# A relational graph layer on one core: more tiles fetched row by row, later stores, an earlier first gather and a reordered end

## The chip, the core and the metric

The kernel runs on one core of one Trainium2 chip. The metric is the device time in microseconds (us) of one execution; lower is better. Several runs are made of a kernel and their median is compared. One more execution is taken by the hardware profiler, which gives the trace read here.

## What is computed

There are N = 12500 nodes with D = 256 features, E = 212500 edges sorted by destination, and R = 8 edge types with a 256x256 weight matrix each.

```python
h = jnp.maximum(_layernorm(x, axis=-1), 0.0)
hx = jnp.einsum('ni,rio->rno', h, weight)
msg = hx[edge_type, src]
agg = jax.ops.segment_sum(msg, dst, num_segments=num_nodes)
node_repr = agg * 0.5 ** 0.5 + h_bias
node_repr = node_repr + (h @ loop_weight) * 0.5 ** 0.5
return x + node_repr
```

The kernel first sums the source rows of each pair (destination, type) and multiplies by the weights afterwards. Both orders give the same result.

## The kernel before

**Tiles.** The edges are cut into units of about 271 and each unit into two tiles of 128 slots; there are 1578 tiles, numbered t. For each tile the 128 source rows (1 KB each) are brought into a tile `msg`. TensorE (PE) multiplies it with a 0/1 matrix made by VectorE (DVE), which sums rows by (destination, type): the "edge sums" of line 1036, four matmuls a tile, 6312 in all. DVE adds each unit's sums into a ring `acc` (L1069). A group of 128 nodes that is complete goes through 18 products with the weights (L1243, two of them the node's own row with `wl`, the "loops"); DVE adds x and the bias (L1231, L1258) and SyncE (SP) stores the rows (L1260 for single groups, L1263 for four groups at once). There are 98 groups.

**How the rows come in.** Most tiles are gathered by one indirect DMA that GpSimd (POOL) issues: L941, in `gather`. One tile in SINGLE (28) is instead "fetched": its 128 rows are copied by 128 plain DMAs of one row each (L970, `load_sources`), 64 issued by SP and 64 by ScalarE's queue (ACT). For every 32 rows the engine first loads 32 addresses into registers (L962, TENSOR_LOAD). PE waits for the rows of such a tile by a counter (L1033). Fetched tiles begin when their row table is normalised and stored in `h32`; gathers of earlier tiles read `x`, and DVE and ACT normalise these tiles in place (L830 to L874).

**Who may run ahead.** One loop over t writes all engines' instructions in one order; every engine executes its own in that order. At step t the gathers up to `goal(t)` are written, which is 64 tiles ahead (AHEAD) up to t = 170, then one tile less every 5 steps down to 24 (NEXT), and towards the end (1578 - t) // 5 down to 8 (CLOSE). Each gather also waits until the last finished unit ahead of its step is summed (L950). The `msg` tiles are a ring of 33 pairs. A fetched tile takes its pair of buffers FAR tiles ahead at the latest, its first rows are written HOLD (8) steps later, four instructions a step for each of the two queues.

**Around it.** Indices come in blocks of 128 units: SP loads `nat_s`, `nat_d` and `nat_t` (L407), then small "spans" transfers follow (L419), eight a block on ACT's queue, for the first such block on SP's. DVE turns them into gather addresses in some 70 small steps (`background`), and in the last block fills the unused part first (L402 to L404). The table of a block's source rows is `gidx`. For the first block it needs a load, a cast, a transposition on PE and a cast (L391, L468, L428, L432).

Of the kernel before, what the change touches and what calls it, by code (L numbers as in the profile page):

```python
# [12 lines left out]
I32 = mybir.dt.int32  # L13
# [47 lines left out]
NEXT = 24  # L61
CLOSE = 8

SINGLE = 28
FETCH = 4
SOURCES = 32
BY_SP = (0, 2)
HOLD = 8
FAR = 36
COUNTERS = 4  # L70
LANDINGS = 68

# [23 lines left out]
PREP = 232  # L96
LOADED = 20
EARLY = 30
SETTLE = 4
ROOM = 5  # L100
SHARE = 1.15
# [148 lines left out]
def kernel(  # L250
# [78 lines left out]
    with ExitStack() as main:  # L329
# [31 lines left out]
        added, zeroed, listed = {}, {}, set()  # L361
        single, fetches = {}, {SP: [], ACT: []}
        counters = [tc.alloc_semaphore(f"rows{i}") for i in range(COUNTERS)]
        fetched, summed = {}, {}
        landings = [tc.alloc_semaphore(f"landed{i}") for i in range(LANDINGS)]
# [17 lines left out]
                runs[kind] = (key, count)  # L383
            return i

        def load_indices(b):

            nat = {name: ep.tile([P, WIDE + 1], I32, name=f"nat_{name}") for name in "std"}
            if b == 0:
# [9 lines left out]
            nat["spans"] = small.tile([P, 2], I32, name="spans")  # L399
            if b == NB - 1:  # L400
                for name in "std":
                    nc.vector.memset(nat[name], N if name == "d" else 0)  # L402
                nc.vector.memset(nat["spans"][:, 0:1], 0)
                nc.vector.memset(nat["spans"][:, 1:2], N + SPAN - (E - spans[-1]))  # L404
# [10 lines left out]
            queue = nc.scalar if b > 1 else nc.sync  # L415
            for k, e in enumerate(spans):
                n = min(TURN, rows_ - k * TURN)
                both = 2 if e + SPAN < E else 1
                queue.dma_start(nat["spans"][k * TURN : k * TURN + n, :both], bass.AP(  # L419
                    tensor=dst.tensor, offset=dst.offset + e, ap=[[0, n], [SPAN, both]]))  # L420
            return nat

# [374 lines left out]
        def prepare(b):  # L797

            got = {}
            return [  # L800
                lambda: got.update(load_indices(b)), *sources(b, got), *last_edges(b, got),
                *columns(b, got), *places(b, got), *(verdict(got) if b == NB - 1 else [])]


# [105 lines left out]

        def single_rows(t):

            return (t % SINGLE == SINGLE - 1 and t + 2 * NEAR < NT
                    and state["h32"] is not None and t // QUAD * QUAD >= state["h32"] + LATE + AHEAD)

        def begin_fetch(t):

            if t not in msg:
                room(t - t % PAIR)
            fetched[t] = len(fetched)  # L920
            for k, r in enumerate(range(0, P, SOURCES)):
                engine = SP if k in BY_SP else ACT
                fetches[engine].append((
                    done["tile"] + HOLD,
                    lambda r=r, engine=engine: load_sources(t, r, engine)))

        def gather(t):
            if t % PAIR == 0 and t not in msg:
                room(t)
            if t % QUAD:  # L930
                kind[t] = kind[t - 1]
            else:
                kind[t] = "h" if state["h32"] is not None and t >= state["h32"] + LATE else "x"
# [7 lines left out]
            i = nc.gpsimd.indirect_dma_start(  # L941
                out=msg[t], out_offset=None, in_=table[:, :],
                in_offset=bass.IndirectOffsetOnAxis(ap=gidx[b][:, at : at + 1], axis=0))
# [269 lines left out]
        def wrap(g):  # L1213
# [3 lines left out]
            tc.add_manual_dep(i.ins, added[plan.last[g]].name, SYNC_DEP, reason="sums complete")  # L1217
            nc.vector.memset(acc[:, :, :, RING : RING + WIN], 0.0)

        def group_work(g):  # L1220

            d0 = plan.starts[g]
# [10 lines left out]
            def product(r, c, g=g):  # L1233
                n = plan.ends[g] - plan.starts[g]
                if (r, c) == (R, 0):
                    got["out", g] = outs[g % 2][:, 0, :]
                if r == R:
                    while ("self", g) not in got:
# [12 lines left out]
                    tc.add_manual_dep(i.ins, added[plan.last[g]].name, SYNC_DEP, reason="sums complete")  # L1251

            def finish():
                q, k = divmod(g, XG)
                rows_ = got["x", q]
                if g != final:
                    biased(g)
                nc.vector.tensor_add(rows_[:n, k, :], rows_[:n, k, :], got["out", g][:n])  # L1258
                if XG * (q + 2) >= plan.NG or n < P:
                    nc.sync.dma_start(out[d0 : d0 + n], rows_[:n, k, :])  # L1260
                elif k == XG - 1:
                    first = plan.starts[XG * q + shorts(q)]
                    nc.sync.dma_start(  # L1263
                        out[first : d0 + n].rearrange("(k p) d -> p k d", p=P), rows_[:, shorts(q) :, :])
                b = g + SLOTS
                q, k = divmod(b, XG)
                if b < plan.NG:
# [18 lines left out]
                    work.append((0.55, lambda r=r, c=c: product(r, c)))  # L1286
            work.append((0.0, last))
            if final is not None and g == final - 1:
                work.append((0.0, lambda: biased(final)))
                for c in range(KC):  # L1290
                    work.append((0.55, lambda c=c: product(R, c, final)))
            return work

        with tc.manual_schedule():

            load = prepare(0)
            load[0]()
            for i in range(STAGED):
                load_rows(i)
            make_identity(nc, ident)  # L1300
# [12 lines left out]
            for f in load[1 : 1 + head]:  # L1313
                f()
            for t in range(min(STARTED, NT)):
                gather(t)
            gathered = min(STARTED, NT)

# [34 lines left out]
            for i in range(2, FIRST):  # L1353
                norm_rows(i)
            after += close()
            for f in load[1 + head :]:
                f()
            after.pop(0)()
            ahead = prepare(1)
            ahead[0]()  # L1360
            nc.vector.memset(acc[:, :, :, RING:].rearrange("p c r d -> p (c r) d"), 0.0)
            for g in range(min(CLEARED, plan.NG)):
                clear(g)
# [28 lines left out]

            def blocks_ahead(t):
                for b in range(1, NB):
                    if t == max(0, PAIR * (RAW + P * (b - 1)) - PREP):
                        for k, f in enumerate(prepare(b) if b > 1 else ahead):
                            if b > 1 or k:
                                background.append((t + ((LOADED if b > 1 else EARLY) + k if k else 0), f))
                        background.sort(key=lambda a: a[0])

            begun = {}
# [44 lines left out]
            for t in range(NT):  # L1446
# [87 lines left out]
                step()  # L1534
            while held():
                advance(None)
            state["general"] = nc.values_load(flag[0:1, 0:1], min_val=0, max_val=1)
            while queue or late:
                if late:
                    late.pop(0)[1]()  # L1540
                else:
                    queue.pop(0)[3]()


    with tc.If(state["general"]):
# [26 lines left out]
```

## Time and profile before

| what | value |
|---|---|
| median of 3 runs | 1940.45 us (1939.35 to 1941.13) |
| the profiled execution, its own time | 1939.95 us |
| its span in the trace | 1938.2 us |
| mean granted TensorE clock | 0.955 |
| PE / DVE / POOL busy, share of the span | 87% / 68% / 75% |
| POOL gathers | 88 from `x`, 1440 from `h32` |
| rows fetched one by one | 3200 by SP, 3200 by ACT: 50 tiles |

The span is 1.75 us shorter than the execution's own time, and that time is 0.5 us below the median. A row of the timeline reads: start in us from the span's start, length in us (of the whole row, where instructions were merged), engine, line, operation, output<-input, count, and in brackets the engine's idle time before it with what ended it. A "q" behind an engine is its sequencer: the issuing of DMAs and loading of registers, which the busy shares leave out.

### The profile page before, as it was taken

To read this page: it belongs to the slowest core of one execution; us is meant where nothing else is said; L and a number is where in the kernel's file an instruction comes from. 1 tells how busy PE (TensorE), PEld (TensorE's weight loads), DVE (VectorE), ACT (ScalarE), POOL (GpSimd) and SP (SyncE) were. 2 spreads that over 40 slices of the span, in tenths; PEclk is the share of its full clock that TensorE was granted. 3 is DMA by queue.
4 is the path that set the end of the run, shared out by engine and by line. 5 is a ranking of instruction groups with operands and counts; after the bars stand their busy time and mean duration, and the time that the engine had idled before them with its cause. 6 is when DMAs were issued, how large, how long until landed. Compare 5 with 4: busy or idle time off the path is not lost.

```text
span 1938.2 us, 40494 instructions
## 1 busy us (share of the span) xinstructions
PE 1693.9 (87%) x10152; PEld 1455.2 (75%) x10152; DVE 1315.0 (68%) x3304; ACT 136.4 (7%) x290; POOL 1453.3 (75%) x1554
## 2 busy tenths in 40 slices
PE   2368999999898899889899989898898989899998
PEld 1357889899887787777777778677777778777887
DVE  7879668976667865657766557775566786565543
ACT  6974000000000000000000000000000000000000
POOL 7777777777777777777777777777777777777775
PEclk9568999999999999999999999999999999999999
DMA  9964444444454444453444444444444444444432
GB/s 319 385 216 138 138 132 131 142 134 143 121 154 131 121 142 131 122 150 111 141 132 121 141 132 130 134 118 142 131 120 136 128 135 132 123 141 127 132 118 87
DMA packets 158466, 279.13 MB, mean 144 GB/s; under 512 B 35487, under 2 KB 109330, under 8 KB 158226
## 3 DMA queue, kind: packets, MB, share of 16 engines
q0 software_dynamic: 73344, 200.38, 35.5%
q1 hardware_dynamic: 76744, 72.84, 12.0%
q10 hardware_dynamic: 8138, 3.30, 0.9%
q8 instruction: 80, 1.31, 0.3%
q14 instruction: 160, 1.31, 0.2%
HBM read 250.78 MB, written 25.60 MB: 143 GB/s over the span
## 4 chain that ended last, share of the span: by engine, by line
PE 37%; DMA 22%; POOL 19%; DVE 9%; issue 9%; ACT 3%; SPq 1%; DVEq 0%; POOLq 0%; ACTq 0%; PEldq 0%
DMA msg<-h,gidx 20%; POOL msg L941 19%; PE po L1243 19%; PE ps L1036 17%; DVE acc L1069 2%; ACT msg L874 1%; DVE oh L998 1%; DVE stats L830 1%; SPq L970 1%; DVE acc L1111 1%; ACT xt L874 1%; DVE moves L456 1%; DMA w<-in_L_gnn_weight_dram 1%; DMA xt<-in_x_dram 1%; PE pt L1093 1%
## 5 line engine op out<-in xcount | busy, mean ns | idle before, releaser
L941 POOL DMA_INDIRECT msg<-h,gidx x1440 | 1367.7, 950 | 439.9 <-issue 374.9
L1036 PEld LDWEIGHTS ps<-oh,msg 128*128 128x128 f32 x6312 | 924.9, 197 | 380.0 <-DMA msg<-h,gidx 247.0
L1036 PE MATMUL ps<-oh,msg 128*128 128x136 f32 (+1 forms) x6312 | 1001.9, 289 | 198.8 <-DMA msg<-h,gidx 122.9
L1243 PE MATMUL po<-w,acc 128*128 128x256 f32 (+1 forms) x3136 | 888.7, 389 | 8.7 <-DVE acc L1069 8.3
L1069 DVE TENSOR_TENSOR acc<-acc,ps 128x352 f32 x789 | 408.2, 517 | 387.5 <-PE ps L1036 376.6
L1243 PEld LDWEIGHTS po<-w,acc 128*128 128x128 f32 (+1 forms) x3136 | 519.1, 193 | 47.5 <-issue 11.9
L1111 DVE SCALAR_TENSOR_TENSOR acc<-types,pt 128x256 f32<-128x256 bf16 x720 | 259.6, 414 | 65.5 <-PE pt L1093 55.5
L998 DVE TENSOR_TENSOR oh<-fixed,cols 128x544 f32<-128x544 f32 x395 | 282.7, 716 | 0.0
L1243 PE MATMUL po<-wl,self_t 128*128 128x256 f32 (+1 forms) x392 | 113.5, 415 | 7.9 <-DVE self_t L1098 3.0
L941 POOL DMA_INDIRECT msg<-in_x_dram,gidx x88 | 83.7, 951 | 28.6 <-issue 23.4
L1243 PEld LDWEIGHTS po<-wl,self_t 128*128 128x128 f32 (+1 forms) x392 | 72.4, 206 | 17.2 <-DVE self_t L1098 4.4
L1231 DVE TENSOR_TENSOR xr<-xr,po 128x256 f32<-128x256 f32 (+1 forms) x98 | 40.6, 414 | 16.1 <-PE po L1243 16.1
L1165 DVE CAST types<-pt 128x512 bf16<-128x512 f32 x23 | 15.9, 690 | 50.8 <-PE pt L1161 50.8
L1258 DVE TENSOR_TENSOR xr<-xr,po 128x256 f32<-128x256 f32 (+1 forms) x98 | 41.2, 421 | 10.6 <-PE po L1243 7.3
L874 ACT ACTIVATE msg<-msg,shift,rstd 128x256 f32<-128x256 f32 x88 | 44.8, 587 | 5.0 <-DVE stats L838 3.4
L456 DVE TENSOR_SCALAR moves<-fixed 128x271 int32<-128x271 int32 (+1 forms) x90 | 40.7, 452 | 3.8 <-DVE acc L1069 2.4
L1093 PE MATMUL pt<-ident,hr 128*128 128x128 f32 (+1 forms) x196 | 38.5, 279 | 5.4 <-DVE self_t L1098 2.4
L1098 DVE COPY self_t<-pt 128x256 f32<-128x256 f32 (+1 forms) x98 | 40.8, 416 | 2.8 <-PE ps L1036 1.8
L458 DVE COPY_PREDICATED fixed<-moves,fixed 128x311 int32<-128x311 int32 (+14 forms) x90 | 38.0, 422 | 3.1
L874 ACT ACTIVATE xt<-xt,shift,rstd 128x256 f32<-128x256 f32 x66 | 33.7, 587 | 10.4 <-DVE shift L871 10.4
L1093 PEld LDWEIGHTS pt<-ident,hr 128*128 128x128 f32 (+1 forms) x196 | 25.6, 150 | 7.6 <-DVE self_t L1098 2.5
L1149 DVE TENSOR_TENSOR of<-pt,line 22x512 bf16<-22x512 f32 x23 | 15.7, 682 | 20.7 <-PE pt L1142 20.6
(168 smaller groups left out, 368.1 us busy)
## 6 DMA issues: line engine op xcount, KB each, us to landing
msg<-h ACTq DMA_DIRECT2D x3200, 1.0 KB
msg<-h SPq DMA_DIRECT2D x3200, 1.0 KB
msg<-h,gidx POOLq DMA_INDIRECT x1440
hr<-h SPq DMA_DIRECT2D x23, 512.0 KB
xr<-in_x_dram SPq DMA_DIRECT2D x23, 512.0 KB
out_dram<-xr SPq DMA_DIRECT2D x22, 512.0 KB
xt<-in_x_dram SPq DMA_DIRECT2D x16, 512.0 KB
h<-xt SPq DMA_DIRECT2D x16, 512.0 KB
```

Source lines behind the costliest of these rows:

```text
L456: nc.vector.tensor_single_scalar(m, packed[:, :n], 1 << (bit + k), op=ALU.bitwise_and)
L874: nc.scalar.activation(row, row, AF.Relu, bias=shift[:n, j : j + 1], scale=rstd[:n, j : j + 1])
L941: i = nc.gpsimd.indirect_dma_start(out=msg[t], out_offset=None, in_=table[:, :], in_offset=bass.IndirectOffsetOnAxis(ap=gidx[b][:, at : at ...
L998: j = nc.vector.tensor_tensor(o[:, k : k + v, :i, :width], iota_f[:, :width].unsqueeze(1).unsqueeze(1).to_broadcast([P, v, i, width]), of. ...
L1036: j = nc.tensor.matmul(ps[:, c, first : first + width], m[:, c * P : (c + 1) * P], o[:, :width], start=(i == 0 and c == 0), stop=(end and ...
L1069: i = nc.vector.tensor_tensor(a, a, ps, op=ALU.add)
L1093: in_run("turns", nc.tensor.transpose(pst[:, c, :n], rows_[:n, c * P : (c + 1) * P], ident[:n, :n]), c == KC - 1)
L1098: nc.vector.tensor_copy(got["self", g][:, :, :n], pst[:, :, :n])
L1111: i = nc.vector.scalar_tensor_tensor(acc[:, :, r, s0 : s0 + n], of, float(r + 1), pst[:, :, :n], op0=ALU.is_equal, op1=ALU.mult)
L1231: nc.vector.tensor_add(rows_[:n, k, :], rows_[:n, k, :], outs[g % 2][:n, 1, :])
L1243: i = nc.tensor.matmul(got["out", g][:n], lhs, rhs, start=(r == R and c == 0), stop=(r == R - 1 and c == KC - 1))
L1258: nc.vector.tensor_add(rows_[:n, k, :], rows_[:n, k, :], got["out", g][:n])
```

## The change

Seven things change. (1) SINGLE goes from 28 to 24, and the fetched tile is the one with t % 24 = 23; the first one is tile 119 (before: 167), the last one 1559 (before: 1539). The first fetched tile is issued by SP alone. (2) FAR goes from 36 to 44. (3) The stores of four groups, and of the short first group, are not written at once but put in a list and written STORE = 44 tiles later. (4) The "spans" of a block are two transfers instead of up to eight, always on SP's queue; in the last block DVE's fills are written 40 tiles ahead of the loads. (5) The first two gathers take their indices from a small tile `direct`, which ACT's queue loads straight from `src`, instead of `gidx`. (6) The last group's loop products are written ahead of the products of the group before it, behind the finish of the group before that. (7) The stores of groups 95 and 96, the last but two and the last but one, are written when all tiles are, and wait for the last edge sums.

```diff
-SINGLE = 28
+SINGLE = 24
+TURN_AT = 23
-FAR = 36
+FAR = 44
+STORE = 44
+FILLED = 40
...
+            whole = sum(e + SPAN < E for e in spans[: rows_ // TURN])
+            for i in range(2 if whole else 0):
+                nc.sync.dma_start(nat["spans"][: whole * TURN, i : i + 1], bass.AP(
+                    tensor=dst.tensor, offset=dst.offset + spans[0] + i * SPAN,
+                    ap=[[SPAN, whole], [0, TURN], [1, 1]]))
...
         def single_rows(t):
-            return (t % SINGLE == SINGLE - 1 and t + 2 * NEAR < NT
-                    and state["h32"] is not None and t // QUAD * QUAD >= state["h32"] + LATE + AHEAD)
+            return (t % SINGLE == TURN_AT and t + 2 * NEAR < NT
+                    and state["h32"] is not None and t // QUAD * QUAD >= state["h32"] + 2 * NEAR - QUAD)
...
-                engine = SP if k in BY_SP else ACT
+                engine = SP if k in BY_SP or not fetched[t] else ACT
...
+            of = direct[:, i : i + 1] if t < PAIR else gidx[b][:, at : at + 1]
             i = nc.gpsimd.indirect_dma_start(
                 out=msg[t], out_offset=None, in_=table[:, :],
-                in_offset=bass.IndirectOffsetOnAxis(ap=gidx[b][:, at : at + 1], axis=0))
+                in_offset=bass.IndirectOffsetOnAxis(ap=of, axis=0))
...
+        def behind(i):
+            tc.add_manual_dep(i.ins, latest["unit"], SYNC_DEP, reason="behind the last edges")
...
                 if (r, c) == (R, 0):
+                    while g == final and final - 2 not in finished:
+                        late.pop(0)[1]()
...
-                if XG * (q + 2) >= plan.NG or n < P:
+                if final is not None and g in (final - 2, final - 1):
+                    alone = rows_[:n, k, :]
+                    stores.append((NT, lambda: behind(nc.sync.dma_start(out[d0 : d0 + n], alone))))
+                elif XG * (q + 2) >= plan.NG:
                     nc.sync.dma_start(out[d0 : d0 + n], rows_[:n, k, :])
+                elif n < P:
+                    short = rows_[:n, k, :]
+                    stores.append((done["tile"] + STORE, lambda: nc.sync.dma_start(out[d0 : d0 + n], short)))
                 elif k == XG - 1:
                     first = plan.starts[XG * q + shorts(q)]
-                    nc.sync.dma_start(
-                        out[first : d0 + n].rearrange("(k p) d -> p k d", p=P), rows_[:, shorts(q) :, :])
+                    to, of = out[first : d0 + n].rearrange("(k p) d -> p k d", p=P), rows_[:, shorts(q) :, :]
+                    stores.append((done["tile"] + STORE, lambda: nc.sync.dma_start(to, of)))
...
             if final is not None and g == final - 1:
+                work = [(0.55, lambda c=c: product(R, c, final)) for c in range(KC)] + work
                 work.append((0.0, lambda: biased(final)))
-                for c in range(KC):
-                    work.append((0.55, lambda c=c: product(R, c, final)))
...
+                nc.scalar.dma_start(direct, src[:U].rearrange("(i p) -> p i", p=P))
...
+                while stores and stores[0][0] <= t:
+                    stores.pop(0)[1]()
                 fetch(FETCH)
```

What this makes of the order, at three places. POOL's own order, from its set-up on (`direct` is the new index tile, `h_57` the table `h32`), before:

```order
L1302 IOTA iota_i 128x512
L1304 IOTA tid 128x1
L1305 IOTA tid 128x6
L1307 MEMSET wraps 128x1 x17
L941 DMA msg<-in_x_dram,gidx 128x256 x88
L941 DMA msg<-h_57,gidx 128x256 x1440
```

and now:

```order
L1335 IOTA tid 128x1
L1336 IOTA tid 128x6
L1338 MEMSET wraps 128x1 x17
L956 DMA msg<-in_x_dram,direct 128x256 x2
L956 DMA msg<-in_x_dram,gidx 128x256 x86
L956 DMA msg<-h_57,gidx 128x256 x1429
```

POOL has 1517 gathers instead of 1528, so 61 tiles are fetched instead of 50.

SP's order where its first fetched rows stand (`hr` and `xr` are rows of four groups that come in, `out_dram<-xr` are stores), before:

```order
L1186 DMA hr<-h_57 128x3x256
L1260 DMA out_dram<-xr 84x256
L1186 DMA hr<-h_57 128x4x256
L1186 DMA xr<-in_x_dram 128x4x256
L1186 DMA hr<-h_57 128x4x256
L1263 DMA out_dram<-xr 128x3x256
L1186 DMA hr<-h_57 128x4x256
L962 TENSOR_LOAD single
L970 DMA msg<-h_57 1x1024 x32
```

and now, first where the rows begin and then where the first store stands:

```order
L1201 DMA hr<-h_57 128x3x256
L1201 DMA hr<-h_57 128x4x256
L1201 DMA xr<-in_x_dram 128x4x256
L1201 DMA hr<-h_57 128x4x256
L977 TENSOR_LOAD single
L985 DMA msg<-h_57 1x1024 x32
```

```order
L977 TENSOR_LOAD single
L985 DMA msg<-h_57 1x1024 x11
L1288 DMA out_dram<-xr 84x256
L985 DMA msg<-h_57 1x1024 x20
L1201 DMA hr<-h_57 128x4x256
```

The first two stores stood ahead of the first row; now the first store stands behind 139 rows, between the rows of the second fetched tile.

PE's order in the last tiles (`po_134` and `po_135` are the two output banks; `ps` edge sums), before:

```order
L1243 MATMUL po_134<-wl,self_t 128x256 x2
L1243 MATMUL po_134<-w,acc 128x256 x2
L1036 MATMUL ps_122<-oh,msg 128x136 x2
L1243 MATMUL po_134<-w,acc 128x256 x4
L1036 MATMUL ps_122<-oh,msg 128x104 x2
L1243 MATMUL po_134<-w,acc 128x256 x4
L1036 MATMUL ps_119<-oh,msg 128x136 x2
L1243 MATMUL po_134<-w,acc 128x256 x3
L1036 MATMUL ps_119<-oh,msg 128x104 x2
L1243 MATMUL po_134<-w,acc 128x256 x3
L1036 MATMUL ps_120<-oh,msg 128x136 x2
L1243 MATMUL po_135<-wl,self_t 128x256 x2
```

and now:

```order
L1264 MATMUL po_135<-wl,self_t 128x256 x2
L1264 MATMUL po_134<-wl,self_t 128x256 x2
L1051 MATMUL ps_122<-oh,msg 128x136 x2
L1264 MATMUL po_134<-w,acc 128x256 x4
L1051 MATMUL ps_122<-oh,msg 128x104 x2
L1264 MATMUL po_134<-w,acc 128x256 x4
L1051 MATMUL ps_119<-oh,msg 128x136 x2
L1264 MATMUL po_134<-w,acc 128x256 x3
L1051 MATMUL ps_119<-oh,msg 128x104 x2
L1264 MATMUL po_134<-w,acc 128x256 x3
L1051 MATMUL ps_120<-oh,msg 128x136 x2
L1264 MATMUL po_134<-w,acc 128x256 x2
```

The two loop products of the last group moved five tiles' sums ahead, and two weight products of the group before it took their place. Everything else stands on PE and DVE in the order of before, except the last block's fills on DVE.

More of the change, by code (lines that the diff above doesn't have):

```diff
@@ L360 @@
         firsts, stops, loops, marked, typed, gidx, col = {}, {}, {}, {}, {}, {}, {}
-        added, zeroed, listed = {}, {}, set()
-        single, fetches = {}, {SP: [], ACT: []}
+        added, zeroed, listed, finished = {}, {}, set(), set()
+        single, fetches, stores = {}, {SP: [], ACT: []}, []
         counters = [tc.alloc_semaphore(f"rows{i}") for i in range(COUNTERS)]
@@ L384, in in_run, with room_for_indices, load_indices @@
             return i
-        def load_indices(b):
+        def room_for_indices(b):
             nat = {name: ep.tile([P, WIDE + 1], I32, name=f"nat_{name}") for name in "std"}
+            if b:
+                nat["spans"] = small.tile([P, 2], I32, name="spans")
+            if b and b == NB - 1:
+                end = E - (RAW * U + (b - 1) * P * EDGES)
+                for name in "std":
+                    nc.vector.memset(nat[name], N if name == "d" else 0)
+                nc.vector.memset(nat["spans"][:, 0:1], 0)
+                nc.vector.memset(nat["spans"][:, 1:2], N + SPAN - ((end - 1) % SPAN + 1))
+            return nat
+        def load_indices(b, nat):
             if b == 0:
@@ L1253, in finish @@
             def finish():
+                finished.add(g)
                 q, k = divmod(g, XG)
@@ L1296 @@
             load = prepare(0)
+            direct = const.tile([P, PAIR], I32, name="direct")
+            with nc.allow_non_contiguous_dma(reason="one unit's indices, a column a tile"):
+                nc.scalar.dma_start(direct, src[:U].rearrange("(i p) -> p i", p=P))
             load[0]()
+            load[1]()
             for i in range(STAGED):
@@ L1312 @@
             head = len(sources(0, {}))
-            for f in load[1 : 1 + head]:
+            for t in range(PAIR):
+                gather(t)
+            for f in load[2 : 2 + head]:
                 f()
-            for t in range(min(STARTED, NT)):
+            for t in range(PAIR, min(STARTED, NT)):
                 gather(t)
@@ L1355 @@
             after += close()
-            for f in load[1 + head :]:
+            for f in load[2 + head :]:
                 f()
@@ L1360 @@
             ahead[0]()
+            ahead[1]()
             nc.vector.memset(acc[:, :, :, RING:].rearrange("p c r d -> p (c r) d"), 0.0)
@@ L1536 @@
                 advance(None)
+            while stores:
+                stores.pop(0)[1]()
             state["general"] = nc.values_load(flag[0:1, 0:1], min_val=0, max_val=1)
@@ L1542 @@
                     queue.pop(0)[3]()
+                while stores:
+                    stores.pop(0)[1]()
     with tc.If(state["general"]):
```

23 lines of the change are left out of this document (10 added, 13 removed).

## The prediction

> **What bounds the kernel now.** I read the page's busy times first, then the list of waits, then the timeline of the engine that never waits.
>
> ```profile
> PE 1693.9 (87%) x10152; PEld 1455.2 (75%) x10152; DVE 1315.0 (68%) x3304; ACT 136.4 (7%) x290; POOL 1453.3 (75%) x1554
> L941 POOL DMA_INDIRECT msg<-h,gidx x1440 | 1367.7, 950 | 439.9 <-issue 374.9 <-PE ps L1036 48.2 <-PE pt L1093 4.9
> L941 POOL DMA_INDIRECT msg<-in_x_dram,gidx x88 | 83.7, 951 | 28.6 <-issue 23.4 <-DVE bound_o L1325 2.1 <-ACT rstd L866 0.9
> ```
>
> PE looks like the bound with 87%, POOL with 75% does not. But POOL's idle time comes in pieces of one size:
>
> ```profile
> POOL msg L941 <- issue: 398.4, 1306, 0.3
> POOL msg L941 <- PE ps L1036: 48.5, 159, 0.3
> POOL msg L941 <- ACT msg L874: 2.4, 6, 0.9
> ...
> POOL msg L941 <- DVE bound_o L1325: 2.1, 1, 2.1
> ```
>
> The last column is the longest wait: 0.3 us, whoever is named, which is the gap that every gather has. Only two are longer: 2.1 us ahead of the first gather, and one of 0.9. So POOL issues gathers back to back over the whole span. The timeline shows the first, the one stop, and the last:
>
> ```profile
> 4.72 1.11 POOL L941 DMA_INDIRECT msg<-in_x_dram,gidx  x1 [2.10 <-DVE bound_o L1325]
> ...
> 164.18 0.95 POOL L941 DMA_INDIRECT msg<-h,gidx  x1 [0.30 <-issue]
> 166.02 0.94 POOL L941 DMA_INDIRECT msg<-h,gidx  x1 [0.89 <-ACT msg L874]
> ...
> 1921.51 0.95 POOL L941 DMA_INDIRECT msg<-h,gidx  x1 [0.30 <-issue]
> ```
>
> How many gathers and edge sums (4 matmuls a tile) fall in a stretch says who leads; x is the count. For L1036, PE:
>
> ```profile
> 0.00:165.90 165.90, 57.44 (x260) 53.10 (x260) 0.71 0.88 292
> 165.90:450.00 284.10, 162.63 (x1113) 162.36 (x1112) 0.99 0.47 133
> 450.00:500.00 50.00, 28.33 (x196) 28.11 (x194) 1.00 0.49 141
> ```
>
> and for L941, POOL, in the same stretches:
>
> ```profile
> 0.00:165.90 165.90, 121.73 (x128) 0.71 0.88 292
> 165.90:450.00 284.10, 215.05 (x226) 0.99 0.47 133
> 450.00:500.00 50.00, 37.83 (x40) 1.00 0.49 141
> ```
>
> At 165.9 us 128 gathers are out and PE has summed 65 tiles: POOL stands at its limit of 64 tiles ahead, and that is the stop of 0.89 us. From there to the end 1400 gathers follow in 1399 intervals: (1921.51 - 166.02) / 1399 = **1.2548 us a gather**. The time is thus made of three parts: PE's start up to tile 63, which fixes the gather at 166.02; POOL's pace; and the tail behind the last gather, 1938.2 - 1921.5 = 16.7 us. After about 500 us PE only follows:
>
> ```profile
> PE ps L1036 <- DMA msg<-h,gidx: 122.2, 210, 2.9
> ```
>
> This is PE's wait for gathered rows between 500 and 1900 us: 122.2 of 1400 us, so 8.7% of its time is spare.
>
> **The change part by part.** *Fetched tiles.* Of 1578 tiles 1517 are gathered instead of 1528. Of the 11 fewer, one (tile 119) lies ahead of the stop at tile 128 and ten behind it: fetched there are now 60 tiles, 50 before. Ten gathers by 1.2548 us are **12.5 us**, all on the path as long as POOL stays the bound.
>
> *First gathers, and tile 119.* POOL's set-up ends 2.1 us ahead of the first gather (the bracket at 4.72), so at most 2.1 us can be won; nothing, or a loss, if `direct` lands after 4.72. I take 1.5, nearer to the full gap, as the index load it replaces is one load instead of a load, two casts and a transposition. Tile 119 gives 1.25. Neither is worth anything: POOL then reaches tile 128 up to 3.35 us sooner and waits there for tile 63's sums, which do not depend on it. What they depend on:
>
> ```profile
> 147.59 0.43 DVE L456 TENSOR_SCALAR moves<-fixed 128x271 int32<-128x271 int32 x1
> ...
> 157.81 1.13 DVE L1069 TENSOR_TENSOR acc<-acc,ps 128x352 f32 x2
> 158.36 1.22 PE L1243 MATMUL po<-w,acc 128*128 128x256 f32 x2 [6.51 <-DVE acc L1069]
> ```
>
> DVE works through ten microseconds of index steps before the add that PE waits 6.51 us for. The order of DVE and PE is unchanged there. So 0 of 2.75 us are counted; the stop at the gather of tile 128 grows instead.
>
> *Rows: can the queues feed 24 instead of 28?* This decides whether the 12.5 us come.
>
> ```profile
> SPq L1263 <- DVE acc L1069: 185.1, 14, 20.0
> SPq L1263 <- DVE xr L1258: 171.4, 9, 57.1
> ```
>
> SP lost 356.5 us in stores that waited for DVE, with the rows queued behind them. Moved 44 tiles back, these stores find their data ready. What the rows themselves cost, from the timelines of PE, ACT and SP and from the loads' durations (least, median, greatest in ns):
>
> ```profile
> 143.67 0.59 PE L1036 MATMUL ps<-oh,msg 128*128 128x104 f32 x4
> ...
> 204.73 86.65 ACTq L970 DMA_DIRECT2D msg<-h  x192
> 209.71 23.34 SPq L970 DMA_DIRECT2D msg<-h  x64
> ...
> 570.48 36.95 SPq L970 DMA_DIRECT2D msg<-h  x96
> ```
>
> ```profile
> L962 SPq TENSOR_LOAD <-single x100: 2057/2180/3772, 206.9 to 1858.2; - x100
> ```
>
> Undisturbed, 96 rows took 36.95 us with two of their three loads inside; with the third (2.18) that is 39.13, so 64 rows cost 26.1 us. Three transfers of four groups per 64 tiles add 3 x 0.41 (the `xr` row below) x 24/64 = 0.5: **26.6 us of SP a fetched tile**. POOL needs 23 x 1.2548 = 28.86 us for the 23 gathers between: SP has 2.3 us to spare. ACT has its 26.1 alone.
>
> In the stage up to 500 us PE is faster than that: (1113 + 196) / 4 = 327 tiles in 334.1 us, 24.5 us for 24 tiles. There SP loses 2.1 us per fetched tile. Its head start: tile 119's buffers are those of tile 53, free at 144.26; its 128 rows are out at 144.3 + 2 x 26.1 = 196.5; PE comes to it at 165.9 + 54 x 1.022 = 221. Rows land late, too:
>
> ```profile
> 494.53 0.41 SPq L1186 DMA_DIRECT2D xr<-in_x_dram  x1
> ...
> 503.48 1.18 PE L1036 MATMUL ps<-oh,msg 128*128 128x104 f32 x4 [4.94 <-PEq L1033]
> ```
>
> The last row of tile 391 was issued by 494.5 and PE went on at 503.48, 9 us later, 4.94 of them waited. Head start 24.6 - 9 = 15.6 us; at 2.1 us a tile it is gone after 7 fetched tiles, and at tile 383, the 11th behind 119, PE is 7.5 us late. POOL feels that only if it reaches its own limit. At 450 us PE has 343 tiles, POOL 354 gathers and 7 fetched, 361; `goal` allows 374: 13 tiles, 16 us. At 500: 392 against 394 + 9 = 403, allowed 417: 14 tiles, 17.6 us. Two more fetched tiles take 2.5 of it. So **13 us of cover against 7.5 us**: PE stalls (at L1048, the new number of L1033), POOL does not: 0 us. Behind 500 us SP wins back 2.3 us a tile. The cover is used up if SP needs 27.1 us instead of 26.6; each further 0.5 us costs some 5 us.
>
> One page speaks against this part. The Trainium skill, "Perfetto Trace Analysis", section "DMA Instruction — HWDGE (DVE, Sync)", says that the block that generates the descriptors is shared by the sequencers that issue such DMAs and locked for the one that uses it, within the span that the profile reports. By that rule SP's and ACT's rows would take turns; what comes of it is the fourth rival below. The rows quoted here disagree: while SP issued 64 rows in 23.34 us, ACT issued 23.34 / 86.65 x 192 = 52.
>
> *Spans and fills.* SP takes over 10 transfers of about 0.4 us in five blocks, ACT loses 37: 0 us, inside SP's spare. DVE's fills only move.
>
> *The tail.*
>
> ```profile
> 1908.99 0.95 POOL L941 DMA_INDIRECT msg<-h,gidx  x1 [0.30 <-issue]
> 1909.44 0.69 PE L1036 MATMUL ps<-oh,msg 128*128 128x104 f32 x4 [0.71 <-DMA msg<-h,gidx]
> ...
> 1920.60 1.03 PE L1243 MATMUL po<-wl,self_t 128*128 128x256 f32 x4
> 1921.46 4.19 PE L1036 MATMUL ps<-oh,msg 128*128 128x104 f32 x28
> ...
> 1933.48 0.42 DVE L1258 TENSOR_TENSOR xr<-xr,po 128x256 f32<-128x256 f32 x1 [7.27 <-PE po L1243]
> ```
>
> From 1909.44 on PE hardly rests. The last fetched tile now stands 18 gathers before the end instead of 38, so PE has less time to make up for a tile that cost POOL nothing: between 0 and one tile's sums (4.19 / 7 = 0.6 us); I take 0.4 lost. The loops (1.03 us) change places with products: 0. The held stores may give PE the 0.71 us of waiting at 1909.44 or nothing; I take 0, since they are issued 8 us ahead of the last store and cannot delay it.
>
> Sum: -12.5 + 0.4 = -12.1 us against the profiled execution's 1939.95: **1927.9 us**, range of its own 1926.5 to 1930. (The median of the runs shown is 0.5 above that execution, well below 0.2%, 3.9 us, which is about what a measurement can tell from no change.)
>
> **The rivals.** *First: the start counts.* If tile 63 is summed sooner, up to 2.75 us of the early gain stay: 1925.2. For it: the spans leave SP's queue sooner, and SP's loads behind the first store move ahead. Against: PE waits for DVE there, not for SP.
>
> *Second: rows late enough to stop POOL* between tiles 335 and 480. At 27.6 us a tile the lateness exceeds the cover by about 5 us: 1933, at worst 1938. For it: the margin is thin and the traffic of rows grows by 22%. Against: 26.1 was measured with both queues at work.
>
> *Third: the queues lose the pace for good*, and the kernel ends slower. The place is SP's queue at L985. It needs over 28.86 us a tile; at 0.40 us a row it is 64 x 0.40 + 2 x 2.18 + 0.5 = 30.5, 1.64 x 60 = 98 us late at the end, less 15 of head start and 15 of cover: 1996. It turns slower than before at 0.386 us a row; 64 rows and one load in 23.34 us are 0.33.
>
> *Fourth: the two queues exclude each other.* 128 rows of 228 ns (the median in the row below) are 29.2, with SP's transfers 29.7 us a tile: 0.84 x 60 = 50 us late, less 30: 1948.
>
> ```profile
> L970 SPq DMA_DIRECT2D msg<-h x3200: 227/228/1044, 209.7 to 1871.4; - x189
> ```
>
> It would be the page's lock above. The 116 rows counted there would be 26.4 us of issuing within 23.34 us, so it hardly holds.
>
> *Fifth: fewer gathers bring nothing*, because PE is the bound after all: 1940. Against: 8.7% spare, where 0.7% is asked.
>
> **How the numbers follow.** Forecast 0.64, start counts 0.10, rows late 0.14, pace lost 0.06, exclusion 0.02, nothing 0.04. Faster by over 0.2% (below 1936.0): 0.64 + 0.10 + 0.12 = 0.86. Within: 0.02 of the late rows + 0.04 = 0.06. Slower: 0.08. The range 1924 to 1936 holds the first two and most of the third; 0.14 lie above it and little below.
>
> **What would show it.** The two gather lines together x1517, still about 1.255 us apart; the first near 3.2 us; one or two gaps between 158 and 166 us, together some 3 us more than the 0.89 of before, and the gather behind them still at 166; no other gap over 0.4; the last at 1909. SP's list of waits without the 356 us of stores. PE waits at L1048 between 350 and 560 us, of some 5 us each, and none later. I am wrong if POOL stops a second time, if SP's rows cost over 27 us per 64, or if the gather of tile 128 moves.

## The result, and the profile after

The changed kernel takes **1975.3 us** (median of 4 runs, 1973.3 to 1976.3) against 1940.07 us (4 runs): 1.018 times the time before, 95% interval 1.0168 to 1.0193. The forecast was 1927.9; the sign was wrong, and the time stands between the second and the third rival. Its profiled execution took 1976.32 us, span 1974.5.

First the waits of the whole kernel (us in total, times, longest us), then the engines' shares of the chain that ended last:

```profile
POOL msg L956 <- issue: 397.9, 1304, 0.3
PE ps L1051 <- PEq L1048: 181.0, 36, 13.5
POOL msg L956 <- PE ps L1051: 93.2, 157, 6.8
PE ps L1051 <- DMA msg<-h,gidx: 6.1, 7, 1.7
```

```profile
SPq 39%; PE 26%; DMA 14%; issue 9%; DVE 9%; ACT 3%; DVEq 0%; POOL 0%; PEldq 0%; ACTq 0%
```

and the same shares in the kernel before:

```profile
PE 37%; DMA 22%; POOL 19%; DVE 9%; issue 9%; ACT 3%; SPq 1%; DVEq 0%; POOLq 0%; ACTq 0%; PEldq 0%
```

PE hardly waits for gathers any more (122 us between 500 and 1900 us before, 6 in the whole kernel now) but 181 us at L1048 for fetched rows, up to 13.5 us at a time. POOL's longest wait is 6.8 us instead of 2.1. The chain runs through SP's queue, which had 1% of it before. The timeline of POOL shows where the forecast held and where it broke:

```profile
3.69 1.11 POOL L956 DMA_INDIRECT msg<-in_x_dram,direct  x1 [1.06 <-DMA direct<-in_src_dram]
...
163.24 0.95 POOL L956 DMA_INDIRECT msg<-h,gidx  x1 [2.80 <-ACT rstd L880]
164.49 0.95 POOL L956 DMA_INDIRECT msg<-h,gidx  x1 [0.30 <-issue]
165.97 0.94 POOL L956 DMA_INDIRECT msg<-h,gidx  x1 [0.54 <-ACT msg L888]
...
493.57 0.94 POOL L956 DMA_INDIRECT msg<-h,gidx  x1 [6.78 <-PE ps L1051]
497.03 0.94 POOL L956 DMA_INDIRECT msg<-h,gidx  x1 [2.53 <-PE ps L1051]
...
1957.85 0.95 POOL L956 DMA_INDIRECT msg<-h,gidx  x1 [0.30 <-issue]
```

The gather of tile 128 stands at 165.97 (166.02 before). Behind it there are ten gathers fewer, -12.5 us, and 30 new stops that add up to 49 us beyond the usual gap of 0.30: 19.9 us between 407 and 510, 27.1 up to 1900, 2.4 behind. So the last gather moves from 1921.51 to 1957.85, by 36.3, which is 49 - 12.5 but for rounding. From it to the end of the span it is 16.7 us, as before. The stretch from 450 to 500 us shows it, edge sums of L1051 on PE and gathers of L956 on POOL (x is the count; 196 and 40 before):

```profile
450.00:500.00 50.00, 24.69 (x155) 0.93 0.38 104
```

```profile
450.00:500.00 50.00, 28.00 (x30) 0.93 0.38 104
```

A stop of PE's costs more than its length, for PE is slow behind it:

```profile
485.28 0.63 PE L1051 MATMUL ps<-oh,msg 128*128 128x136 f32 x4
...
492.11 1.18 PE L1051 MATMUL ps<-oh,msg 128*128 128x104 f32 x4 [5.34 <-PEq L1048]
```

The granted clock is 1.00 from 470 to 486 us and 0.50 from 492 to 497. Behind 200 us it stands at 0.5 for 243 us in all, in the kernel before for 80. What part of POOL's 49 us of stops comes of the slower clock was not separated.

SP's stores wait no longer, as intended (the two held to the end apart), and between 200 and 1900 us SP hardly rests. Here are two and a half tiles' worth of its timeline, and ACT's beside it.

```profile
SPq L1292 <- DVE acc L1084: 2.8, 7, 0.5
```

```profile
639.68 20.39 SPq L985 DMA_DIRECT2D msg<-h  x45
660.13 0.41 SPq L1201 DMA_DIRECT2D hr<-h  x1
660.63 26.28 SPq L985 DMA_DIRECT2D msg<-h  x64
686.97 0.40 SPq L1201 DMA_DIRECT2D xr<-in_x_dram  x1
687.47 20.50 SPq L985 DMA_DIRECT2D msg<-h  x53
708.06 0.41 SPq L1292 DMA_DIRECT2D out_dram<-xr  x1
711.90 0.27 SPq L985 DMA_DIRECT2D msg<-h  x1
```

```profile
640.00 72.03 ACTq L985 DMA_DIRECT2D msg<-h  x172
```

SP's rows of tile 167 end at 245.6 us, those of tile 1559 at 1928.4: 58 fetched tiles in 1682.8 us, **29.0 us a fetched tile** where the forecast had 26.6 and POOL's 23 gathers leave 28.86. In the mean a row holds SP for 262 ns (235 before) between 220 and 1860 us.

### The profile page after: what moved, and what is told of

It reads as the page before. It is cut to its first block, busy times and chain, and to the rows that moved or that the text cites. A ratio compares the mean times of both kernels' runs of the same rounds, so it can differ in the third digit from the quotient of the medians.

```text
span 1974.5 us, 43352 instructions
## 1 busy us (share of the span) xinstructions
PE 1659.5 (84%) x10152; PEld 1504.6 (76%) x10152; DVE 1311.8 (66%) x3304; ACT 136.3 (7%) x290; POOL 1442.5 (73%) x1543
## 3 DMA queue, kind: packets, MB, share of 16 engines
q10 hardware_dynamic: 7952, 3.95, 1.2%
## 4 chain that ended last, share of the span: by engine, by line
SPq 39%; PE 26%; DMA 14%; issue 9%; DVE 9%; ACT 3%; DVEq 0%; POOL 0%; PEldq 0%; ACTq 0%
SPq L985 31%; PE po L1264 14%; DMA msg<-h 11%; PE ps L1051 11%; SPq L977 7%; DVE acc L1084 2%; ACT msg L888 1%; DVE acc L1126 1%; DVE stats L844 1%; DMA msg<-h,gidx 1%; DVE oh L1013 1%; DMA xt<-in_x_dram 1%; DVE moves L469 1%; DMA w<-in_L_gnn_weight_dram 1%; ACT xt L888 1%
## 5 line engine op out<-in xcount | busy, mean ns | idle before, releaser
L956 POOL DMA_INDIRECT msg<-h,gidx x1429 | 1356.9, 950 | 488.0 <-issue 374.4
L1051 PEld LDWEIGHTS ps<-oh,msg 128*128 128x128 f32 x6312 | 964.5, 202 | 348.5 <-PEq L1048 193.9
L1051 PE MATMUL ps<-oh,msg 128*128 128x136 f32 (+1 forms) x6312 | 979.8, 288 | 257.2 <-PEq L1048 181.0
L1264 PE MATMUL po<-w,acc 128*128 128x256 f32 (+1 forms) x3136 | 905.5, 395 | 19.7 <-DVE acc L1084 19.2
L1264 PEld LDWEIGHTS po<-w,acc 128*128 128x128 f32 (+1 forms) x3136 | 528.1, 197 | 63.0 <-DVE acc L1084 25.2
L956 POOL DMA_INDIRECT msg<-in_x_dram,gidx x86 | 81.6, 949 | 26.2 <-issue 23.1
```

The costliest lines, as they stand in the source:

```text
L956: i = nc.gpsimd.indirect_dma_start(out=msg[t], out_offset=None, in_=table[:, :], in_offset=bass.IndirectOffsetOnAxis(ap=of, axis=0))
L1051: j = nc.tensor.matmul(ps[:, c, first : first + width], m[:, c * P : (c + 1) * P], o[:, :width], start=(i == 0 and c == 0), stop=(end and ...
L1264: i = nc.tensor.matmul(got["out", g][:n], lhs, rhs, start=(r == R and c == 0), stop=(r == R - 1 and c == KC - 1))
```

## The experiments

Two questions: is it SP's queue, or another part of the change, or the rows as such; and what is it that takes 29.0 us. Each kernel was timed beside the kernel before on the same chip; ratios are to that.

### All of the change with one tile in 28

```diff
-SINGLE = 24
-TURN_AT = 23
+SINGLE = 28
+TURN_AT = 27
```

> All of the change, but one tile in 28 fetched (52 tiles instead of 61). Theory A, SP's queue cannot supply a fetched tile in the time that 23 gathers take (28.9 us measured against 28.86 and against the 28.1 that a shrinking lead leaves): at 28 there are 27 gathers, 33.9 us, between two fetched tiles, POOL stops at tile 128 only, and one gather fewer than before stands behind that stop: 1938.7 us. Rival B, every fetched row slows the gathers and sums beside it through shared memory traffic, whoever issues it: two of the eleven extra tiles are left, 2/11 of the 48 us: 1946. Rival C, another part of the change (spans on SP, later stores, first gathers, tail) costs the time: about 1975 or more.

Measured: 1941.31 us against 1943.24, ratio 0.999 (0.998 to 0.9999). Theory A's -1.25 us came as -1.9; rivals B (1946) and C (1975) fall. So the other six edits cost nothing that shows, and the gain is about what the one gather fewer is worth. POOL's longest wait for sums is the usual gap, and PE waits for gathers again:

```profile
PE ps L1051 <- DMA msg<-h,gidx: 137.4, 236, 2.7
POOL msg L956 <- PE ps L1051: 47.3, 155, 0.3
```

### The kernel before with one tile in 24

```diff
-SINGLE = 28
+SINGLE = 24
```

> The kernel before with one tile in 24 fetched and nothing else (59 tiles). Theory A: SP's rows still stand behind stores that wait for DVE, some 5 us a fetched tile on top of 26 to 27, so SP is later than in the changed kernel: 1985 to 2040 us. Rival B (traffic): two fetched tiles fewer than in the changed kernel, 1966. Rival C (the other parts cost the time): 1930.

Measured: 1966.37 us, ratio 1.0117 (1.01 to 1.0134): faster than the changed kernel, though its stores stand where they stood before. Theory A is wrong about the stores. Its waits (from 200 us on) say why:

```profile
SPq L1263 <- DVE xr L1258: 67.9, 7, 56.9
SPq L1263 <- DVE acc L1069: 25.1, 9, 7.0
```

```profile
PE ps L1036 <- PEq L1033: 176.4, 42, 10.3
```

Of the 356 us that SP spent in such stores, 93 are left: SP had waited there because it was early. When the rows are late, the stores' data are ready. A fetched tile takes the same 29.1 us (tile 167's rows end at 233.9, tile 1559's at 1923.6). It has two fetched tiles fewer, 119 and 143, and so is through with tile 167 some 12 us sooner. Rival B's figure for this kernel, 1966, came true, but its 1946 for the kernel ahead of it did not.

### Spans, stores and rows taken off SP

If SP's own issuing were the bound, each of these would bring back most of the loss. The spans on ACT's queue:

```diff
-                nc.sync.dma_start(nat["spans"][...
+                nc.scalar.dma_start(nat["spans"][...
```

> The changed kernel with the spans of a block on ACT's queue again. Theory A: SP sheds ten transfers that took 14.4 us of its time, and up to 18.6 us by which the rows behind them were longer than 228 ns; the kernel ends 14 to 33 us sooner, 1942 to 1961. Rival B: SP's queue does not matter, 1975.

Measured: 1974.36 us, ratio 1.0163 (1.0146 to 1.018). SP shed the transfers, and its rows became longer elsewhere (264 ns in the mean): nothing won that can be told from the changed kernel. Theory A as put falls.

The stores of four groups, and in the same way that of the short first group, on ACT's queue:

```diff
-stores.append((done["tile"] + STORE, lambda: nc.sync.dma_start(to, of)))
+stores.append((done["tile"] + STORE, lambda: nc.scalar.dma_start(to, of)))
```

> The changed kernel with the late stores of four groups issued by ACT's queue. SP sheds 9.6 us of issuing. Theory A1, a row is longer when its own queue has just taken a transfer of 512 KB: SP's rows behind stores lose their 51 us of excess and the kernel ends 40 to 48 us sooner, 1928 to 1937, unless ACT becomes the late queue. Theory A2, a row is longer when any queue moves such a transfer: 10 us sooner, 1965. Rival B: 1975.

Measured: 1988.94 us, ratio 1.0231 (1.0214 to 1.0248). Both A1 and A2 fail, and the 0.5% that it lost beside the changed kernel is not explained by what follows.

No stores of four groups at all (those rows of the output stay unwritten):

```diff
-stores.append((done["tile"] + STORE, lambda: nc.sync.dma_start(to, of)))
+pass
```

> The changed kernel without the stores of four groups: 22 of the 29 stores are left out and those rows of the output stay unwritten. Theory I: SP sheds 9.6 us of issuing and up to 51 us by which the rows behind stores were longer, 1928 to 1940. Theory S: the excess is backlog of rows and comes back behind other rows; only what a store itself takes of the server is won, 22 x 0.4 = 9 us: 1962 to 1970.

Measured: 1972.11 us, ratio 1.016 (1.0142 to 1.0179). Theory I's 1928 to 1940 is out; theory S is nearer, but even its 9 us did not come.

Every twelfth fetched tile with 96 rows by ACT and 32 by SP:

```diff
-engine = SP if k in BY_SP or not fetched[t] else ACT
+engine = SP if (k in BY_SP and (k or fetched[t] % 12 != 6)) or not fetched[t] else ACT
```

> The changed kernel, but in every twelfth fetched tile ACT issues 96 rows and SP 32. Theory I, SP's own issuing is the bound (29.0 us a fetched tile): SP falls to 27.85 and ACT rises from 27.2 to 28.3, both below the 28.1 to 28.9 that is needed, and the kernel is bound by POOL again or nearly: 1930 to 1945 us. Theory S, the rows of both queues pass one server behind the queues that takes 29.0 / 128 = 0.227 us a row, whoever issues it: the number of rows is the same, a fetched tile still takes 29 us, 1970 to 1977.

Measured: 1968.7 us, ratio 1.0143 (1.0124 to 1.0161), 24 us above theory I's range and 1 us below theory S's. SP issued 160 rows fewer, and each of its rows became longer: 274 ns in the mean, ACT's 259 (262 and 256 in the changed kernel). What is taken from one queue is lost in it again. So the rows are held up behind the queues.

### One queue alone

```diff
-SINGLE = 24
-TURN_AT = 23
+SINGLE = 40
+TURN_AT = 39
-engine = SP if k in BY_SP or not fetched[t] else ACT
+engine = SP
```

> The changed kernel with one tile in 40 fetched and all 128 rows of it issued by SP, none by ACT, so that SP's issuing hardly rests. Theory S: one queue alone offers a row each 0.34 us to a server that takes 0.227, so nothing piles up: issuing a row keeps SP for 0.235 us in the mean as in the kernel before, 128 rows with four loads and transfers take 128 x 0.337 + 4 x 2.3 + 1.7 = 54 us. Theory I, with the longer rows a property of one busy queue beside its transfers: 0.262 us a row, 57.5 us a fetched tile. Supply is 39 x 1.2548 = 48.9 us, so the kernel is slow by either, 2000 us or more; the size is in the profile.

Measured once: 2150.08 us; the answer is in the profile. SP hardly rests here either, with the same transfers between its rows; a row holds it for 233 ns in the mean, and a fetched tile takes 53.3 us. The line's durations (least/median/greatest ns), here and in the changed kernel:

```profile
L985 SPq DMA_DIRECT2D msg<-h x4736: 224/228/887, 144.1 to 2113.4; - x198
```

```profile
L985 SPq DMA_DIRECT2D msg<-h x3968: 224/228/5566, 144.4 to 1928.2; - x199
```

The medians are the same; the long rows are gone with ACT's. Theory S's 0.235 and 54 us a tile are right, theory I's 0.262 and 57.5 are not. And something else went: the median time from the issue of a gather to its landing, of the changed kernel and of this one.

```profile
msg<-h,gidx POOLq DMA_INDIRECT x1429, 9.3
```

```profile
msg<-h,gidx POOLq DMA_INDIRECT x1453, 2.8
```

Gathers are POOL's, on a queue of their own, and they land 6.5 us later when both other queues issue rows. The trace has 16 increments of the semaphore for a gather. Worked out from it, for those gathers of which all 16 are recorded: the median time from the gather's end on POOL to the 15th and to the last increment (us), beside the mean time in which one row was issued by both queues together.

```
                        350 to 600 us              900 to 1300 us
kernel                  us a row  15th  last       us a row  15th  last
before (28)             0.228     1.8   7.2        0.268     1.8   3.7
changed (24)            0.220     1.8   9.2        0.228     1.8   9.0
all, one in 28          0.226     1.8   8.8        0.265     1.8   3.7
before, one in 24       0.225     1.8   8.7        0.224     1.8   9.1
spans on ACT            0.219     1.8   9.0        0.227     1.8   8.9
stores on ACT           0.222     1.8   9.5        0.230     1.8   9.1
no stores               0.221     1.8   9.4        0.226     1.8   9.2
uneven                  0.224     1.8   9.0        0.224     1.8   8.8
SP alone, one in 40     0.415     1.8   1.8        0.417     1.8   1.8
one in 26               0.225     1.8   8.6        0.238     1.8   7.2
half rows               0.220     1.8  10.8        0.227     1.8  10.5
28, then 24             0.225     1.8   8.6        0.223     1.8   8.8
```

**Fifteen of sixteen parts of a gather land after 1.8 us in every kernel; one part is late, and the more so the closer the rows come to one in 0.23 us.**

The Trainium skill, "DMA: Bandwidth & Descriptors", section "Why a DMA increments its semaphore by 16 and not by 1", says that each of the 16 DMA engines posts one of a gather's increments, and that a transfer from SP or ACT that isn't split runs on the lowest-numbered engine. The trace agrees as far as it shows: ACT's 3840 rows make 3840 packets of 1024 B and as many of 4 B (7680 of the 7952 below), so a row isn't split, and one increment of sixteen is late. Which number that engine has, the records don't say.

```profile
q10 hardware_dynamic: 7952, 3.95, 1.2%
```

The packets say more. Between 350 and 1860 us of the changed kernel, more than 14 us behind any other transfer, data packets of rows follow each other 3872 times, 2773 times from one queue to the other, and all but three overlap by 12 ns at most: the rows of both queues move one after another. And a row of ACT's begins to move 8.6 us after its issue ended (median, 900 to 1300 us), in the kernel before after 1.5.

However rows, stores and spans are dealt out, the kernels with one tile in 24 fetched issue a row every 0.219 to 0.230 us, and no kernel issues faster. Behind 500 us POOL's 28.86 us for 128 rows would give 0.2255 as well; that the rows are the limit there too is seen from PE, which waits 158.8 us for them between 560 and 1900 us and 3.8 for gathers. That is theory D of the last expectations below: all single rows of both queues pass one DMA engine, which has a queue in front of it, and it takes about 0.225 us for a row beside its sixteenth of the gathers; 128 rows are 28.8 us. What makes up the 0.225 us stays open: without the stores a row took no less (0.221 to 0.226), and why the kernel with the stores on ACT's queue is slower it does not say.

### One tile in 26

```diff
-SINGLE = 24
-TURN_AT = 23
+SINGLE = 26
+TURN_AT = 25
```

> The changed kernel with one tile in 26 fetched, 56 tiles. Supply is 25 x 1.2548 = 31.4 us, less about 0.9 that the shrinking lead takes, 30.5, against 29.0. Both theories: the rows keep up, POOL stops at tile 128 only, and 5 gathers fewer than in the kernel before stand behind that stop: 1933.7. If the rows cost more than 30.5 us a tile even here: 1940 to 1955.

Measured: 1945.86 us, ratio 1.0033 (1.0021 to 1.0045). Missed, by theories I and S alike (it lies in the range that was given for dearer rows, but the rows were not dearer): the supply was reckoned by POOL's pace, but up to 500 us PE passes 26 tiles in 26 x 1.022 = 26.6 us, and the rows take 29. POOL stops there for 14.4 us in all, and nowhere later:

```profile
493.53 0.94 POOL L956 DMA_INDIRECT msg<-h,gidx  x1 [7.81 <-PE ps L1051]
497.98 0.94 POOL L956 DMA_INDIRECT msg<-h,gidx  x1 [3.52 <-PE ps L1051]
```

In the table its queue is full up to 600 us and shrinks later, as a limit between 29 and 31.4 us a tile has it.

### Bytes or rows: half of every row

Only the first 512 B of a fetched row are copied; DVE sets the rest to zero.

```diff
+nc.vector.memset(msg[t][:, D // 2 :], 0.0)
...
-msg[t][r0 + i : r0 + i + 1, :].bitcast(U8), h32_bytes[:, bass.ds(v, D * 4)])
+msg[t][r0 + i : r0 + i + 1, : D // 2].bitcast(U8), h32_bytes[:, bass.ds(v, D * 2)])
```

> The changed kernel with only the first 512 B of every fetched row copied; the other half of such a tile is set to zero by DVE, so the sums of fetched tiles lack half of the features. The number of DMAs and their issuing are the same. If the one DMA engine needs its time for each DMA (two packets, data and semaphore): 29 us a fetched tile as before, 1970 to 1978. If it needs it for the bytes: the rows fit, the sixteenth part of a gather lands within 2 to 4 us instead of 9, and POOL is the bound: 1927 to 1935.

On the chip of this run the kernel before took 2398.85 us and this one 2573.68; nothing is concluded from it. On another:

> The same kernel as the first one with half rows, on another chip. If the one DMA engine needs its time for each DMA: 29 us a fetched tile, 1970 to 1978. If for the bytes: POOL is the bound, 1927 to 1935, and the sixteenth part of a gather lands within 2 to 4 us.

Measured: 1970.73 us, ratio 1.0159 (1.0143 to 1.0174), 0.223 us a row, the last part of a gather after 10 to 11 us. Half the bytes bring nothing: the engine takes its time for each DMA, at least from 512 B to 1024 B.

### A version that goes by the limit

One tile in 28 up to tile 600, where the rows just keep up, then one in 24, paid from the lead that they have there.

```diff
+turn = t % 28 == 27 if t < 600 else t % 24 == 11
-return (t % SINGLE == TURN_AT and t + 2 * NEAR < NT
+return (turn and t + 2 * NEAR < NT
```

> The changed kernel, but one tile in 28 fetched up to tile 600 and one in 24 behind it: 58 tiles fetched, 57 of them behind tile 128 (50 in the kernel before). Theory D, all single rows pass one DMA engine that needs 29.0 us for the rows of a fetched tile beside its share of the gathers: up to tile 600 the sums pass 28 tiles in 28.6 us or more, so the rows just keep up; from there 23 gathers give 28.1 us with the shrinking lead, 0.9 us too little, 40 tiles x 0.9 = 36 us, and the 60 us by which the rows are ahead there pay for it. POOL stops at tile 128 only, 7 gathers fewer: 1939.95 - 8.8 = 1931, 0.995 to 0.996 of before. If the rows cost more or the head start is less: POOL stops late in the kernel, 1935 to 1950.

On the chip where the kernel before took 2398.85 us it took 2507.43, ratio 1.0441: there it loses. In its trace the rows come only every 0.28 to 0.31 us, so the limit of this document is not reached there; why that chip was slow was not studied. On another:

> The same kernel as the one before it, one tile in 28 fetched up to tile 600 and one in 24 behind it, on another chip: on the first one the kernel before took 2399 us instead of 1940, so neither its times nor its profile can be set beside the others. Theory D as there: 1931 us, 0.995 to 0.996 of before; if the rows cost more or the head start is less, 1935 to 1950.

Measured: **1933.29 us against 1939.54, ratio 0.997 (0.9958 to 0.9981)**, 2 us above theory D's figure. The queue of rows is full throughout (table), yet behind the first gather POOL has two longer stops only, one ahead of tile 128 and one at it. In the profiled execution, at 1929.76 us the fastest of the seven, the last gather comes 10.2 us sooner than in the kernel before:

```profile
162.93 0.94 POOL L957 DMA_INDIRECT msg<-h,gidx  x1 [2.43 <-ACT rstd L880]
...
1911.35 0.95 POOL L957 DMA_INDIRECT msg<-h,gidx  x1 [0.30 <-issue]
```

## Why the prediction was wrong

- **POOL as the bound, 1.2548 us a gather, 12.5 us for ten gathers: right.** Behind tile 128 POOL's time is 1389 intervals of 1.2548 us and 49 us of stops.
- **The start and tile 119 count nothing: right.** The first gather came at 3.69 (1.03 us sooner; 1.5 was taken), the stops ahead of tile 128 grew by 2.2 us (2.50 + 0.24 beyond the usual gap, 0.59 before), and the gather of tile 128 stayed.
- **"26.6 us of SP a fetched tile": this step failed.** It was worked out from the issuing of 96 rows between pauses. An issue ends when the DMA is handed over, and behind it stood a queue some 9 us deep. In a kernel whose rows never pause, that queue stays full and the issuing takes the pace of the engine behind it, 29.0 us. "ACT has its 26.1 alone" failed with it: the two queues share that engine. The pace to compare with was a row in 0.225 us for both queues; 28.86 us for 128 rows is 0.2255, and the 24.5 us of the stage up to 500 us is 0.191.
- **The row was there.** The prediction quoted a wait of PE 9 us behind the last row's issue and took it for a fixed delay. It was the depth of the queue: in the kernel before the last part of a gather came after 7.2 us in that stage and after 3.7 later.
- **The argument against the fourth rival held against its lock and not against its price.** It set 116 rows in 23.34 us against 26.4 us of issuing; but a server behind a queue takes such a burst too. That rival's 29.7 us a tile was nearly right, by luck, for there is no sign of a lock: between 220 and 1860 us a row holds SP for 262 and ACT for 256 ns, while each issues one in 0.35 to 0.36 us. The spans overlap, and in 248 pairs of an SP row and an ACT row that overlap by 150 ns or more neither is longer than 235 ns. On this the trace disagrees with the rule that the prediction weighs, of the Trainium skill, "Perfetto Trace Analysis", section "DMA Instruction — HWDGE (DVE, Sync)".
- **The sum up to 500 us was right in its form.** With 29.0 in place of 26.6 it reads: 11 x (29.0 - 24.5) = 49.5, less 15.6 of head start is 34, less 13 of cover is 21 us. Measured: 19.9. The pace put into it was what was off; that the sum comes so near is in part luck, for it has no term for the slower clock behind PE's stops.
- **"Behind 500 us SP wins back 2.3 us a tile", and the break-even of 0.386 us a row: wrong.** At 29.0 against 28.86 SP loses 0.14 us a tile, 6 us over 44 tiles. And POOL's lead shrinks from 24 tiles to 8, 16 x 1.25 = 20 us, which PE has to make up and the rows cannot; the break-even let head start and cover, spent by then, pay for this stage too. Together 26 us; measured 29.5. As a balance of the stage that is near, but it does not say where the stops fall: 24.7 of the 29.5 us come before 1600 us, when the lead is still 24 tiles, and 15.1 of these in clusters at fetched tiles on which SP had spent 33 to 44 us (479, 623, 719, 1247) instead of the mean 29.0. ACT had issued its half of these tiles 34 to 69 us earlier, so SP's other transfers have a part that theory D's mean leaves out; on tile 1247 index transfers kept SP from rows from 1528.4 to 1548.4 us. What made the other three long was not settled. The kernel that dealt 160 of SP's rows to ACT won little by it: 1.0143 instead of 1.0181. A row costs SP 0.36 us from one start to the next, less than that break-even, and the kernel is slower all the same.
- **Stores, spans, tail.** The 356 us of SP's waits went, and nothing hung on them. The spans cost nothing that shows. The tail is as long as before (0.4 us was taken as lost).

## What to carry to other kernels

How long an issue takes says how fast work is handed over, not how fast it is done: before a queue is asked for more, look at how late its transfers land in the busiest stage, part by part, since a mean over 16 DMA engines (46% busy here) hides one that is full. Many small DMAs that aren't split can share one engine whichever queue issues them, so a second queue adds only what that engine has left (here from a row in 0.417 us to one in 0.225); their limit is then a number of DMAs in a time, not of bytes. And a supply has to be measured against the fastest stage of its consumer: a share that the whole kernel could bear (26 tiles) lost in the stage up to 500 us, while a share that changes with the stage won by 0.3%, on one of the two chips it ran on.

## What the runs showed of the hardware

- Single-row DMAs of both queues move one after another, as by one DMA engine, at about 0.225 us each beside the gathers, for 1024 B and for 512 B alike (0.219 to 0.230 in the seven kernels that fetch one tile in 24).
- Rows on SP's and ACT's queues delay POOL's gathers: the last sixteenth lands after 9 to 11 us instead of 1.8. With gathers issued far ahead it costs nothing by itself: in the kernel with 28, then 24 it lands after 8.6 to 8.8 us and POOL stops nowhere behind tile 128.
- The queue in front of that engine held about 9 us of rows; the last part of a gather came at most 13 us after the gather in the two stages of the table, 16 with half rows. With the queue full some issues become longer, but only some: the median stays at 228 ns while the mean goes from 235 to 262.
- While PE stood still from 486.8 to 492.1 us the granted clock fell to 0.5, at 491.5, and stayed there until 498.3.
